# A wait for the gate's weight sums in a graph network's attention

## The chip, the cores and the metric

The kernel runs on one core of a Trainium2 chip. The metric is the time of one execution in device microseconds. Three runs of the kernel before took 2556.47, 2557.34 and 2559.36 us; their median is 2557.34 us.

## The reference

A graph of 1024 nodes with 512 features (all float32) goes through a graph convolution, four transformer layers and a second graph convolution. Around them lie a first normalisation and two residual additions. One layer l, cut to what matters here:

```python
a = attn(ln(h, ln2_w[l], ln2_b[l]), cond, Wq[l], Wk[l], Wv[l], Wo[l])
h = h + a
u = ln(h, ln3_w[l], ln3_b[l]) @ geglu_w[l] + geglu_b[l]   # 512 -> 4096
val, gate = split(u, 2)
h = h + (val * gelu(gate)) @ ffo_w[l] + ffo_b[l]          # 2048 -> 512
```

The attention is a cross attention: the nodes are 16 graphs of 64 nodes each, every graph has its own 256 rows of `cond` (512 features), and keys and values are made from those. There are 8 heads of 64 features. The softmax runs over the 256 rows.

## The kernel before

**The products.** Almost every large product is done by a scheme of Strassen's kind: a 2 x 2 block product takes seven block products in place of eight, in exchange for sums of blocks. Sums of weights are made once per weight. For the keys of one step, `seven` writes seven products into four PSUM banks, named a, b, c and d in the profile (pa_k, pb_k, pc_k, pd_k). PE issues first a, then b, c, d, and then a, c and d again. Between these, other engines take the banks out: ScalarE (ACT) copies a to `s1` (L719), VectorE (DVE) adds b to it (L722, `u_k`), adds c (L725), adds d (L727), and later takes out the second c and d (L733, L735). PE's second product into a bank must wait until the first has been read.

**The attention.** It goes in NG = 8 steps g of two graphs (128 nodes) each. Step g, in the order in which the instructions stand in the program:

- `scores(l, g)`: the score products on PE into four banks, and then, for each bank u, the negated maximum on DVE (L771), the exponentials with their sums on ACT (L776), the reciprocals of the sums on DVE (L779) and two scalings of the probabilities with them on DVE (L781; each is a tensor of 128 x 256 with one factor per row, in place). So a step has eight scalings.
- `kv(l, g + 1)`: keys of the next step (seven products), then a function `between`, then the values of the next step (seven products). So DVE finds the sums of the keys (L722 and on) behind the scalings of this step in its queue.
- `mix(l, g)`: the transposed probabilities times the values.

The function `between` does, in every second step, what is left of two earlier steps: `pair_sums` forms sums of the two steps' outputs on GpSimd (POOL, L846 to L849), and `attn_out_pair` multiplies them with the output projection on PE (banks wab and wcd) and adds the result to h, on DVE (L870 to L881) and POOL (L873, L874, L879, L882). Then DVE makes the next norm's statistics of finished nodes. In step g = NG - 2 = 6 `between` has one task more, ahead of `attn_out_pair`: `geglu_weights(l, 0, *raw)` forms the sums of the first block of the feed-forward part's weights (`wval`, `wgate`, giving `ges`), in four POOL instructions of 128 x 1024 elements (L219 to L222). Their result is first used by PE in the feed-forward part, bank gb. These weights' loads are issued by SP at the beginning of step 6 in program order.

**What sets the order.** Each engine runs its instructions in the order in which the program issues them; between engines semaphores wait for data, and the framework puts those in. The kernel has two means beside: `tc.issue_after` places instructions behind another one in the order, and its own `waiting_for(ins, engine)` gives every instruction that the enclosed code issues on one engine a further dependency, on the instruction `ins`:

Of the kernel before, what the change touches and what calls it, by code (L numbers as in the profile page):

```python
# [14 lines left out]
OP = mybir.AluOpType  # L15
# [8 lines left out]
def gnn_kernel(  # L24
# [26 lines left out]
    nc = tc.nc  # L51
# [29 lines left out]
    @contextmanager  # L81
    def waiting_for(ins, engine):

        traced = nc.cur_bb.bb.instructions
        n = len(traced)
        yield
        for i in traced[n:]:
            if i.engine == engine:
                tc.add_manual_dep(i, ins.ins.name, mybir.DependencyInfo(
                    mybir.DependencyClass.Sync, mybir.DependencyReason.DATA))  # L90

    def bank(name):
        return psum.tile([P, 512], F32, tag="bank", name=name)

    def t512(name, dtype=F32):
        return work.tile([P, 512], dtype, tag="t512", name=name)
# [4 lines left out]
    def slots_of(n, name):  # L101
        return [slot(f"{name}_{i}") for i in range(n)]
# [114 lines left out]
    def sums_of_a(t, a11, a12, a21, a22, s1, s2, s4):  # L217

        t.tensor_tensor(s1, a21, a22, OP.add)  # L219
        t.tensor_tensor(a21, a11, a21, OP.subtract)  # L220
        t.tensor_tensor(s2, s1, a11, OP.subtract)
        t.tensor_tensor(s4, a12, s2, OP.subtract)  # L222
# [37 lines left out]
    def fetch_cond(g):  # L260
        if g < NG:
            raw_conds[g] = [t512(f"cond_{g}_{i}") for i in range(2 * MB)]
            for i, ctile in enumerate(raw_conds[g]):
                nc.sync.dma_start(
                    ctile, cond[2 * g + i // MB, (i % MB) * P:(i % MB + 1) * P, :]
                )
# [19 lines left out]
    conds, left = {}, None  # L286
# [460 lines left out]
    def kv(l, g, wk, wv, between, **also):  # L747
        kT, last_key = keys(l, g, wk)
        between(last_key)
        return kT, values(l, g, wv, **also)  # L750

    def scores(l, g, qT, kT):


        c0 = (g % 4) * P
        probs = []
        banks = [bank(f"sc_{l}_{g}_{u}") for u in range(4)]
        for c2 in range(2):
            for a in range(2):
                for j in range(2):  # L760
                    pj = slice(j * DH, (j + 1) * DH)
                    for b in range(2):
                        with tc.issue_after(mix.last.ins) if g else nullcontext():
                            nc.tensor.matmul(
                                banks[2 * c2 + j][b * NPG:(b + 1) * NPG, a * M:(a + 1) * M],
                                qT[g // 4][c2][pj, a, c0 + b * NPG:c0 + (b + 1) * NPG],
                                kT[c2][pj, a, b * M:(b + 1) * M], start=True, stop=True)
        for u in range(4):
            ps3 = banks[u].rearrange("p (a m) -> p a m", a=2)
            nmax = small.tile([P, 2], F32, tag="nmax", name=f"nmax_{l}_{g}_{u}")  # L770
            nc.vector.tensor_reduce(nmax, ps3, AX.X, OP.max, negate=True)  # L771
            pr = t512(f"pr_{l}_{g}_{u}")
            pr3 = pr.rearrange("p (a m) -> p a m", a=2)
            tot = small.tile([P, 2], F32, tag="tot", name=f"tot_{l}_{g}_{u}")
            for a in range(2):
                nc.scalar.activation(pr3[:, a, :], ps3[:, a, :], AF.Exp,  # L776
                                     bias=nmax[:, a:a + 1], accum_out=tot[:, a:a + 1])
            inv = small.tile([P, 2], F32, tag="inv", name=f"inv_{l}_{g}_{u}")
            nc.vector.reciprocal(inv, tot)  # L779
            for a in range(2):  # L780
                nc.vector.tensor_scalar(pr3[:, a, :], pr3[:, a, :], inv[:, a:a + 1], None, OP.mult)  # L781
            probs.append(pr)
        return probs

# [54 lines left out]
    def pair_sums(l, g, oTs):  # L839

        n = f"{l}_{g}"
        t = nc.gpsimd
        a11, a12, a21, a22 = (halves_of(oT[:, k * M:(k + 1) * M]) for oT in oTs for k in range(2))
        s, more = acc_tile(f"os_{n}"), acc_tile(f"om_{n}")
        s1, s2, s4 = (halves_of(x) for x in (s[:, :M], s[:, M:], more[:, :M]))
        t.tensor_tensor(s1, a21, a22, OP.add)  # L846
        t.tensor_tensor(a21, a11, a21, OP.subtract)
        t.tensor_tensor(s2, s1, a11, OP.subtract)
        t.tensor_tensor(s4, a12, s2, OP.subtract)  # L849
        return [a11, a12, s4, a22, s1, s2, a21], more[:, M:]  # L850

    def attn_out_pair(l, g, left, p1, right):

        n = f"{l}_{g}"
        t = nc.gpsimd
        ab, cd = bank(f"wab_{n}"), bank(f"wcd_{n}")
        a, b, c, d = ab[:, :M], ab[:, M:], cd[:, :M], cd[:, M:]
        h11, h12, h21, h22 = (h[g + i][:, j * M:(j + 1) * M] for i in range(2) for j in range(2))

        def product(i, to, start):  # L860
            multiply(to, left[i], right[i], [(0, P, 0, M)], start)

        kept = acc_tile(f"ou_{n}")
        u2, p7 = kept[:, :M], kept[:, M:]
        product(0, a, True)
        nc.scalar.copy(p1, a)
        product(6, c, True)
        nc.scalar.copy(p7, c)
        product(4, d, False)
        nc.vector.tensor_tensor(h22, d, h22, OP.add)  # L870
        product(5, b, False)
        nc.vector.tensor_tensor(u2, b, p1, OP.add)
        t.tensor_tensor(p7, p7, u2, OP.add)  # L873
        t.tensor_tensor(h22, p7, h22, OP.add)  # L874
        product(1, a, False)
        nc.vector.tensor_tensor(h11, a, h11, OP.add)
        product(3, c, False)
        nc.vector.tensor_tensor(h21, c, h21, OP.add)
        t.tensor_tensor(h21, u2, h21, OP.add)  # L879
        product(2, d, False)  # L880
        nc.vector.tensor_tensor(h12, d, h12, OP.add)  # L881
        t.tensor_tensor(h12, u2, h12, OP.add)  # L882

    def order7(blk, s1, s2, s4):

        return [blk[0], blk[1], s4, blk[3], s1, s2, blk[2]]

    def load_geglu(l, r):
        return [load_w(geglu_w[l][:, r * D:(r + 1) * D], f"wval_{l}_{r}"),
                load_w(geglu_w[l][:, DFF + r * D:DFF + (r + 1) * D], f"wgate_{l}_{r}")]  # L890
# [4 lines left out]
    def geglu_weights(l, r, wval, wgate):  # L895
        s = slots_of(3, f"ges_{l}_{r}")
        sums_of_a(nc.gpsimd, *wval, *wgate, *s)
        return order7([*wval, *wgate], *s)
# [241 lines left out]
    for l in range(L):  # L1140
# [42 lines left out]
        def ln3_norm(*blocks, behind=None):  # L1183
            with tc.issue_after(behind.ins) if behind else nullcontext():
                if blocks:
                    of = [h[nb] for nb in blocks]
                    name = f"ln3_{l}_{blocks[0]}"
                    xns.update(zip(blocks, scaled(of, *moments(of, name), name)))

        def ln3_turn(nb, by=(0, 1)):  # L1190
            turn(xns.pop(nb), ln3T[nb // 4], nb % 4 * P, LN3W + l * KC, LN3B + l * KC,
                 f"ln3_{l}_{nb}", by)
# [8 lines left out]
        for g in range(NG - 1):  # L1201
            kT, v = kv_next
            if g == NG - 2:
                raw = load_geglu(l, 0)
            if l == 0:
                fetch_cond(g + 2)
            probs = scores(l, g, qT, kT)
            ready = [g - 2, g - 1] if g == NG - 2 else [g - 2] if g > 1 else []

            def between(last_key):  # L1210
                nonlocal left
                if len(oTs) == 2:
                    blocks = pair_sums(l, g - 2, oTs)
                    oTs.clear()
                    if g == NG - 2:
                        left = geglu_weights(l, 0, *raw)
                    attn_out_pair(l, g - 2, *blocks, wo7)
                ln3_norm(*ready, behind=last_key)

            if g or l:  # L1220
                kv_next = kv(l, g + 1, wk, wv, between, late=lambda: [ln3_turn(nb) for nb in ready])
            else:
                kv_next = kT_1, values(0, 1, wv)
            save_conds()
            next_cond(l, g + 2)
            for nb in ready:
                if nb >= 4:
                    ln3_sums(nc.gpsimd, nb)
            oTs.append(mix(l, g, probs, v))
# [40 lines left out]
        for r in range(R):  # L1270
# [7 lines left out]
            if r + 1 < R:  # L1278
                raw = load_geglu(l, r + 1)
# [13 lines left out]
            if r + 1 < R:  # L1293
                raw_out = load_out(l, r + 1)
                left = geglu_weights(l, r + 1, *raw)
# [74 lines left out]
```

## Time and profile before

| | |
|---|---|
| median of three runs | 2557.34 us |
| the profiled execution, its own time | 2556.88 us |
| span of the profiled execution | 2555.1 us |
| PE busy (matmuls) | 2516.4 us, 98% of the span |
| DVE busy | 1428.2 us, 56% |
| POOL busy | 646.6 us, 25% |
| ACT busy | 558.0 us, 22% |
| granted clock of PE, mean | 0.996 |

The times in the rows are microseconds from the span's start. A row of a timeline gives the start, the length, the engine, the line of the kernel, the operation and its operands; "x8" says that eight equal instructions that follow each other were merged into one row, and a bracket at the end gives the idle time of the engine before it and what ended it. "PEld" is the loading of weights into PE, which overlaps its matmuls. A name such as pa_k stands for all tiles of that name. "PEclk" or granted clock is the share of PE's full clock that was granted. Layer 0 has its step 6 from about 366 us of the span on, layer 1 from 951, layer 2 from 1545 and layer 3 from 2136.

### The profile page before, as it was taken

To read this page: it belongs to the slowest core of one execution; us is meant where nothing else is said; L and a number is where in the kernel's file an instruction comes from. 1 tells how busy PE (TensorE), PEld (TensorE's weight loads), DVE (VectorE), ACT (ScalarE), POOL (GpSimd) and SP (SyncE) were. 2 spreads that over 40 slices of the span, in tenths; PEclk is the share of its full clock that TensorE was granted. 3 is DMA by queue.
4 is the path that set the end of the run, shared out by engine and by line. 5 is a ranking of instruction groups with operands and counts; after the bars stand their busy time and mean duration, and the time that the engine had idled before them with its cause. 6 is when DMAs were issued, how large, how long until landed. Compare 5 with 4: busy or idle time off the path is not lost. (4 is left out here: it accounts for less than half of the span.)

```text
span 2555.1 us, 32224 instructions
## 1 busy us (share of the span) xinstructions
PE 2516.4 (98%) x12464; PEld 1773.5 (69%) x12464; DVE 1428.2 (56%) x3026; ACT 558.0 (22%) x1318; POOL 646.6 (25%) x539
## 2 busy tenths in 40 slices
PE   8999999999999999999999999999999999999999
PEld 5778886666578886655577887555677887566565
DVE  9655556544664556554474556654475456654561
ACT  7322222111122222111122222111112222211111
POOL 0322234532110012533310003343320002352410
PEclk9999999999999999999999999999999999999999
DMA  5302241111121212010212112110112121111020
GB/s 177 129 38 83 91 139 52 37 50 57 42 83 46 71 34 75 25 54 17 95 38 75 63 63 67 33 54 17 58 66 75 56 77 37 51 33 63 12 87 34
DMA packets 67136, 156.81 MB, mean 61 GB/s; under 512 B 5576, under 2 KB 5904, under 8 KB 66976
## 3 DMA queue, kind: packets, MB, share of 16 engines
q1 hardware_dynamic: 64880, 149.25, 17.9%
q0 software_dynamic: 1376, 4.30, 0.5%
q8 instruction: 103, 1.69, 0.3%
q10 hardware_dynamic: 720, 1.11, 0.1%
q14 instruction: 57, 0.47, 0.1%
HBM read 133.66 MB, written 20.97 MB: 61 GB/s over the span
## 5 line engine op out<-in xcount | busy, mean ns | idle before, releaser
L301 PE MATMUL ga<-ln3T,wval 128*128 128x512 f32 x512 | 233.9, 593 | 0.0
L931 ACT ACTIVATE g<-g,gcols 128x512 f32<-128x512 f32 x128 | 92.3, 721 | 430.9 <-DVE g L944 366.2
L301 PEld LDWEIGHTS ga<-ln3T,wval 128*128 128x128 f32 x512 | 96.0, 190 | 109.9 <-issue 109.1
L776 ACT ACTIVATE pr<-sc,nmax 128x256 f32<-128x256 f32 x256 | 118.2, 474 | 185.4 <-DVE nmax L771 185.4
L846 POOL TENSOR_TENSOR os<-oT 128x256 f32<-128x256 f32 x12 | 8.7, 728 | 566.8 <-DVE oT L821 566.8
L1005 POOL TENSOR_TENSOR hall<-fu,hall 128x512 f32<-128x512 f32 x24 | 30.5, 1270 | 430.5 <-DVE fu L1004 430.5
L301 PE MATMUL pc_k<-ct,wk 128*128 128x256 f32 x512 | 124.8, 388 | 12.4 <-DVE u_k L725 12.4
L301 PE MATMUL pa_v<-wv,ct 128*128 128x256 f32 x512 | 123.1, 379 | 0.0
L301 PE MATMUL pd_k<-ct,wks 128*128 128x256 f32 x512 | 121.9, 381 | 0.0
L301 PE MATMUL fa<-wff,fT 128*128 128x256 f32 x512 | 121.6, 379 | 0.0
L301 PE MATMUL gc<-ln3S,wgate 128*128 128x512 f32 x256 | 120.4, 592 | 1.1 <-DVE gu L941 1.1
L301 PE MATMUL pc_v<-wv,ct 128*128 128x256 f32 x512 | 121.0, 379 | 0.0
L301 PE MATMUL pd_v<-wvs,ct 128*128 128x256 f32 x512 | 121.0, 379 | 0.0
L301 PE MATMUL gd<-ln3T,ges 128*128 128x512 f32 x256 | 120.6, 593 | 0.0
L301 PE MATMUL gb<-ln3S,ges 128*128 128x512 f32 x256 | 120.3, 592 | 0.0
L301 PE MATMUL gc<-ln3T,wgate 128*128 128x512 f32 x256 | 120.3, 592 | 0.0
L301 PE MATMUL gd<-ln3S,ges 128*128 128x512 f32 x256 | 120.3, 592 | 0.0
L301 PE MATMUL pa_k<-ct,wk 128*128 128x256 f32 x480 | 118.0, 389 | 2.1 <-ACT s_k L719 2.1
L301 PEld LDWEIGHTS pc_k<-ct,wk 128*128 128x128 f32 x512 | 99.2, 194 | 27.6 <-DVE u_k L725 13.8
L301 PEld LDWEIGHTS fa<-wff,fT 128*128 128x128 f32 x512 | 97.3, 190 | 21.8 <-issue 9.6
L301 PEld LDWEIGHTS pd_k<-ct,wks 128*128 128x128 f32 x512 | 98.3, 192 | 13.7
L781 DVE TENSOR_SCALAR pr<-pr,inv 128x256 f32<-128x256 f32 x256 | 104.9, 452 | 2.9
(318 smaller groups left out, 4906.0 us busy)
## 6 DMA issues: line engine op xcount, KB each, us to landing
ct<-cond_dram SPq DMA_DIRECT2D x72, 512.0 KB, 4.6
wval<-in_L_gnn_geglu_w_dram SPq DMA_DIRECT2D x32, 512.0 KB, 3.8
wgate<-in_L_gnn_geglu_w_dram SPq DMA_DIRECT2D x32, 512.0 KB, 4.6
wff<-in_L_gnn_ffo_w_dram SPq DMA_DIRECT2D x32, 512.0 KB, 4.7
cond_dram<-ct SPq DMA_DIRECT2D x24, 512.0 KB, 3.0
cond<-in_L_gnn_cond_dram SPq DMA_DIRECT2D x32, 256.0 KB, 4.5
ct<-cond_dram SPq DMA_DIRECT2D x24, 256.0 KB, 4.5
wk<-in_L_gnn_Wk_dram SPq DMA_DIRECT2D x8, 512.0 KB, 5.0
```

Source lines behind the costliest of these rows:

```text
L301: nc.tensor.matmul(at, left[:, k, l0:l1], right[:, k, r0:r1], start=start and n == 0 and k == 0, stop=n == len(cols_of) - 1 and k == 1, sk ...
L776: nc.scalar.activation(pr3[:, a, :], ps3[:, a, :], AF.Exp, bias=nmax[:, a:a + 1], accum_out=tot[:, a:a + 1])
L781: nc.vector.tensor_scalar(pr3[:, a, :], pr3[:, a, :], inv[:, a:a + 1], None, OP.mult)
L846: t.tensor_tensor(s1, a21, a22, OP.add)
L931: nc.scalar.activation(pre, pre, AF.Gelu, bias=gcols[:, cg:cg + 1])
L1005: t.tensor_tensor(h21, halves_of(u2), h21, OP.add)
```

## The change

`scores` keeps its last scaling, and in step 6 `between` puts the four weight sums under `waiting_for` with it. When `between` runs, `scores(l, 6)` has been issued and `scores(l, 7)` has not, so the instruction that is kept is the eighth scaling of step 6. The order of the instructions on each of the five engines is that of before; only the first of the four sums in each layer waits for a further semaphore, DVE's.

```diff
             for a in range(2):
-                nc.vector.tensor_scalar(pr3[:, a, :], pr3[:, a, :], inv[:, a:a + 1], None, OP.mult)
+                scores.last = nc.vector.tensor_scalar(pr3[:, a, :], pr3[:, a, :], inv[:, a:a + 1],
+                                                      None, OP.mult)
             probs.append(pr)
         return probs
...
                     if g == NG - 2:
-                        left = geglu_weights(l, 0, *raw)
+                        with waiting_for(scores.last, mybir.EngineType.Pool):
+                            left = geglu_weights(l, 0, *raw)
                     attn_out_pair(l, g - 2, *blocks, wo7)
```

## The prediction

> **What bounds the kernel now.** I read the page first: busy time by engine. TensorE (PE) works through nearly the whole span, so time is to be had only where PE stands still or runs slow.
>
> ```profile
> span 2555.1 us, 32224 instructions
> PE 2516.4 (98%) x12464; PEld 1773.5 (69%) x12464; DVE 1428.2 (56%) x3026; ACT 558.0 (22%) x1318; POOL 646.6 (25%) x539
> ```
>
> The span less PE's busy time leaves 38.7 us in which PE is idle. The list of PE's waits says for whom; its columns are the total, the number of times and the longest.
>
> ```profile
> PE pc_k L301 <- DVE u_k L725: 12.4, 3, 5.3
> ...
> PE pa_k L301 <- ACT s_k L719: 2.1, 1, 2.1
> ```
>
> Four stalls, 14.5 us, all in the key products. The timeline of PE shows where: in layers 1, 2 and 3, in the attention's step g = 6 (the last but one), between the first product of the keys (pa_k) and the first one of the paired output projection (wab). I quote these two for layer 0, for step 4 of layer 1, then for step 6 of layers 1, 2 and 3 with the stalls between them (start, length, instruction, idle time before it).
>
> ```profile
> 367.46 1.99 PE L301 MATMUL pa_k<-ct,wk 128*128 128x256 f32 x8
> ...
> 376.19 1.89 PE L301 MATMUL pc_k<-ct,wk 128*128 128x256 f32 x8
> 377.92 1.89 PE L301 MATMUL pd_k<-ct,wks 128*128 128x256 f32 x8
> ...
> 379.65 1.03 PE L301 MATMUL wab<-wo,oT 128*128 128x256 f32 x4
> ...
> 886.22 1.99 PE L301 MATMUL pa_k<-ct,wk 128*128 128x256 f32 x8
> ...
> 898.41 1.03 PE L301 MATMUL wab<-wo,oT 128*128 128x256 f32 x4
> ...
> 953.18 1.99 PE L301 MATMUL pa_k<-ct,wk 128*128 128x256 f32 x8
> ...
> 967.41 3.78 PE L301 MATMUL pc_k<-ct,wk 128*128 128x256 f32 x8 [5.33 <-DVE u_k L725]
> ...
> 973.40 1.03 PE L301 MATMUL wab<-wo,oT 128*128 128x256 f32 x4
> ...
> 1546.78 1.99 PE L301 MATMUL pa_k<-ct,wk 128*128 128x256 f32 x8
> ...
> 1556.06 3.66 PE L301 MATMUL pa_k<-ct,wk 128*128 128x256 f32 x8 [2.11 <-ACT s_k L719]
> 1561.43 1.99 PE L301 MATMUL pc_k<-ct,wk 128*128 128x256 f32 x8 [1.71 <-DVE u_k L725]
> ...
> 1564.99 1.03 PE L301 MATMUL wab<-wo,oT 128*128 128x256 f32 x4
> ```
>
> The table by stretches takes the same piece in the four layers, the last one layer 3 (length, then PE busy, weight loads, DVE, ACT, POOL; then the granted clock).
>
> ```profile
> 367.46:379.65 12.19, 12.19 (x61) 10.74 (x57) 7.56 (x19) 5.01 (x18) 7.71 (x7) 1.00 1.01 335
> 953.18:973.40 20.22, 14.89 (x60) 12.31 (x57) 14.84 (x19) 5.01 (x18) 11.41 (x7) 0.83 0.23 64
> 1546.78:1564.99 18.21, 14.39 (x61) 11.66 (x58) 14.97 (x19) 5.01 (x18) 11.36 (x7) 0.91 0.22 64
> 2138.36:2158.21 19.85, 14.51 (x60) 12.08 (x57) 14.84 (x19) 5.01 (x18) 11.41 (x7) 0.83 0.23 61
> ```
>
> The same work takes 12.19 us undisturbed, both in layer 0 and in step 4 of layer 1 (898.41 - 886.22), and 18 to 20 us in the three others. Part of the excess is idle time, part is a slow clock after it: eight matmuls that take 1.89 us take 3.78 and 3.66 behind the gaps.
>
> Why DVE is late there: its own timeline and POOL's in layer 1.
>
> ```profile
> 954.93 2.85 DVE L781 TENSOR_SCALAR pr<-pr,inv 128x256 f32<-128x256 f32 x2
> ...
> 958.37 4.19 DVE L781 TENSOR_SCALAR pr<-pr,inv 128x256 f32<-128x256 f32 x2
> ...
> 962.67 2.57 DVE L781 TENSOR_SCALAR pr<-pr,inv 128x256 f32<-128x256 f32 x2
> ...
> 965.35 0.62 DVE L781 TENSOR_SCALAR pr<-pr,inv 128x256 f32<-128x256 f32 x2
> ...
> 966.67 0.69 DVE L725 TENSOR_TENSOR u_k<-pc_k,u_k 128x512 f32<-128x512 f32 x1
> ```
>
> ```profile
> 955.23 2.40 POOL L219 TENSOR_TENSOR ges<-wgate,wgate 128x1024 f32<-128x1024 f32 x1
> 957.71 2.35 POOL L220 TENSOR_TENSOR wgate<-wval,wgate 128x1024 f32<-128x1024 f32 x1
> 960.02 2.39 POOL L221 TENSOR_TENSOR ges<-ges,wval 128x1024 f32<-128x1024 f32 x1
> 962.49 2.34 POOL L222 TENSOR_TENSOR ges<-wval,ges 128x1024 f32<-128x1024 f32 x1
> ```
>
> Two scalings of probabilities (L781) take 0.62 us alone and up to 4.19 beside the four weight sums: a scaling that meets a running sum gets through only about when that sum ends (at 957.6, 960.1, 962.4 and 964.8). The additions that free PE's banks (L722, L725) queue behind them. The sums are not hurt: 2.34 to 2.40 us each.
>
> **The change, part by part.** It adds one condition, to the four weight sums on POOL in step 6: they wait for the last L781 of that step. No instruction is added, removed or reordered, on any queue; DMA issues and SP's and POOL's queues keep their order.
>
> *Layer 0: nothing.* The lines are POOL's and DVE's there.
>
> ```profile
> 375.23 2.35 POOL L219 TENSOR_TENSOR ges<-wgate,wgate 128x1024 f32<-128x1024 f32 x1 [4.25 <-issue]
> 377.67 2.36 POOL L220 TENSOR_TENSOR wgate<-wval,wgate 128x1024 f32<-128x1024 f32 x1
> ...
> 382.42 2.35 POOL L222 TENSOR_TENSOR ges<-wval,ges 128x1024 f32<-128x1024 f32 x1
> 384.74 0.72 POOL L873 TENSOR_TENSOR ou<-ou 128x256 f32<-128x256 f32 x1
> ...
> 387.26 0.73 POOL L882 TENSOR_TENSOR hall<-ou,hall 128x256 f32<-128x256 f32 x1 [0.33 <-DVE hall L881]
> ```
>
> ```profile
> 372.35 0.62 DVE L781 TENSOR_SCALAR pr<-pr,inv 128x256 f32<-128x256 f32 x2
> ...
> 378.12 0.69 DVE L733 TENSOR_TENSOR kT<-pc_k,u_k 128x512 f32<-128x512 f32 x1 [2.76 <-PE pc_k L301]
> ...
> 382.51 0.42 DVE L872 TENSOR_TENSOR ou<-wab,om 128x256 f32<-128x256 f32 x1 [1.97 <-PE wab L301]
> ```
>
> The last scaling ends at 372.97, the sums begin at 375.23 anyhow (they were idle 4.25 us, which I read as their weights' late arrival). So layer 0 already runs what the change makes of the others, later still. I give times from the start of pa_k (367.46) from here on: last scaling done at +5.5, sums from +7.8 to +17.3.
>
> *Layers 1 to 3: the stalls go.* With POOL silent, the four pairs of scalings take 0.62 us each, and the last is done near +5.5 as in layer 0. L725 then ends well ahead of +8.7, where PE comes to the second pc_k (376.19 in layer 0). So each piece falls to 12.19 us:
> 20.22 - 12.19 = 8.03 (layer 1), 18.21 - 12.19 = 6.02 (layer 2), 19.85 - 12.19 = 7.66 (layer 3), together 21.71 us. Of that 14.5 us is idle time and the other 7.2 the slow clock.
>
> At the clock stands the one place where a page and a row part. In layer 2 a gap of 2.11 us was enough: the next eight matmuls took 3.66 us in place of 1.89. The Trainium skill (TensorE: Matmul & The Clock Gate, section "What's actually happening") says the gate falls to half rate after at least one idle window of about 3.4 us, which the 2.11 us do not fill. The trace does not bear out the plain reading of that rule. By it the slow stretch of layer 2 would have another cause and stay, as the fourth rival below.
>
> *What the wait pushes back.* The sums take 382.42 + 2.35 - 375.23 = 9.54 us, so in layers 1 to 3 they run from about +5.6 to +15.2, not from +2. Behind them in POOL's queue stand the additions of the paired output projection (L873, L874, L879, L882), whose first DVE input (L872) is there at 382.93, that is +15.5, and the last of which feeds the statistics of the next norm. In layer 0 the sums end 2 us later than that and L882 still waited 0.33 us for DVE, and PE lost nothing. Cost: 0. Without that cover (sums ending past about +17.6) each us would be a us on the path.
>
> The sums' results are first used by PE in gb:
>
> ```profile
> 429.95 1.88 PE L301 MATMUL gb<-ln3S,ges 128*128 128x512 f32 x4
> ```
>
> That is 50 us after wab, far beyond a delay of 3.5 us. SP's loads follow PE and DVE, not these sums.
>
> *What the moved sums now lie beside.* No longer L781, but L725, L727, L733 and L735, which read PSUM. Below, the cost is 0: L733 took its 0.69 us in layer 0 beside L220, and a gain is excluded because 12.19 is PE's unbroken time. Above, one sum each, 2.35 us. I take 0, since the row is of the same instructions beside the same sums.
>
> *The sum.* 2556.88 us is the time of the profiled execution (its span is 2555.1). 2556.88 - 21.71 = 2535.2. The median shown, 2557.34, lies 0.46 above; I give 2535.4, between the two. What is late next in these pieces: nothing, PE runs through.
>
> **The rivals.**
> 1. *The moved sums block the additions.* For it: POOL does stop DVE here. Against it: L733 beside L220. If every L725 and L727 waited for the running sum, L725 would wait for the end of L219 (+8.0) and end near +8.7, just in time, and L727 behind L220 near +11.1, some 0.6 us after PE wants its bank at +10.5 (377.92); with L735 and the projection's additions caught too I put it at one sum a layer, 3 x 2.35 = 7 us: 2542.
> 2. *Slower: the sums end too late.* Place: L882 in POOL's queue, then norm and transposes. It costs from an end at about +17.6 on, and outweighs the gain only beyond 21.71/3 = 7.2 us more, when the sums begin after about +15. The wait would have to be let go 10 us after the last scaling, by some later DVE instruction. A release at +20 gives an end at +29.5, 12 us a layer: 36 - 21.7 = 14 slower, 2571. For it: waits are counted by engine, and I can't see the release. Against it: DVE's order puts L781 ahead of all of L722 to L735.
> 3. *It does nothing*, because the weights land after the scalings as in layer 0: 2557. Against it: in layers 1 to 3 the sums start with no idle time ahead of them.
> 4. *The slow stretch of layer 2 stays*: 6.02 - 2.11 - 1.71 = 2.20 us kept, 2537.6. Against it: clock 1.00 in layer 0's same piece, 0.83 and 0.91 only where PE had stood.
>
> **How the numbers follow.** Forecast 0.86, rival 1 0.06, rival 4 0.03, rival 2 0.03, rival 3 0.02. The time is the forecast's, 2535.4. Its own spread is some 1.5 to 3 us, since the three runs before lie between 2556.47 and 2559.36; one sum's length in two layers more above gives 2532.5 to 2541, which holds forecast and rival 4 and the lighter half of rival 1. Faster by over 0.2% (5.1 us, about what a measurement of this kernel can tell from no change): 0.86 + 0.06 + 0.03 = 0.95. Within it: 0.02. Slower: 0.03.
>
> **What would show it.** Right: in layers 1 to 3 every L781 of step 6 is near 0.3 us; the sums start within 0.3 us of the last one's end; pa_k to wab is 12.19 us four times; no wait of PE for L725 is left; PE's idle time is near 24 us; L882's idle time before it is still for L881. Wrong: L725 or L727 longer than 0.7 us beside the sums (rival 1), idle time of DVE's statistics for L882 that grows with PE idle at the transposes (rival 2), sums that start late for another reason, or a new stall further on, as where loads now come too late for a PE that runs 21.7 us ahead.

## The result and the profile after

The changed kernel takes 2533.2 us (median of six runs, 2532.9 to 2534.0); the kernel before takes 2556.9 us (2556.2 to 2559.4, six runs, the three shown above among them). The ratio is 0.991, with a 95% interval of 0.989 to 0.992. The change saves about 23.7 us. The forecast was 2535.4 in a range of 2532.5 to 2541.

The profiled execution took 2532.89 us with a span of 2531.1. The page, busy time by engine:

```profile
span 2531.1 us, 32228 instructions
...
PE 2506.6 (99%) x12464; PEld 1768.6 (70%) x12464; DVE 1403.6 (55%) x3026; ACT 557.3 (22%) x1318; POOL 646.0 (26%) x539
```

The same 12464 matmuls are 9.8 us shorter in sum (2516.4 before), and PE's idle time is 24.5 us in place of 38.7. DVE also lost 24.6 us of "busy" time with the same 3026 instructions, which was waiting booked as work. The list of PE's waits (total, times, longest) has no row for L725 or L719 any more. What is left of it that lies in the layers:

```profile
PE fd L301 <- DVE fs L978: 1.9, 1, 1.9
...
PE gc L301 <- DVE gu L942: 1.1, 1, 1.1
```

(L978 was L977 before: from L782 on the lines of the changed kernel are one higher, from L1217 on two.) The table by stretches, from pa_k to wab in step 6 of layers 0 to 3 (length, then PE busy, weight loads, DVE, ACT, POOL; then the granted clock):

```profile
367.07:379.26 12.19, 12.19 (x60) 10.75 (x57) 7.54 (x19) 5.00 (x18) 7.72 (x7) 1.00 1.00 335
952.62:964.81 12.19, 12.19 (x60) 10.75 (x57) 7.18 (x19) 5.00 (x18) 8.91 (x6) 1.00 0.32 95
1538.18:1550.38 12.20, 12.20 (x61) 10.75 (x58) 7.05 (x19) 5.00 (x18) 8.79 (x6) 1.00 0.32 96
2123.75:2135.94 12.19, 12.19 (x61) 10.75 (x58) 7.18 (x19) 5.00 (x18) 8.91 (x6) 1.00 0.31 96
```

All four pieces are now equal to layer 0's, at full clock, where layers 1 to 3 had 20.22, 18.21 and 19.85. DVE's timeline and then POOL's, layer 1 (pa_k starts at 952.62):

```profile
957.13 0.62 DVE L781 TENSOR_SCALAR pr<-pr,inv 128x256 f32<-128x256 f32 x2
957.66 0.68 DVE L722 TENSOR_TENSOR u_k<-pb_k,s_k 128x512 f32<-128x512 f32 x1
958.45 0.69 DVE L725 TENSOR_TENSOR u_k<-pc_k,u_k 128x512 f32<-128x512 f32 x1
959.83 0.69 DVE L727 TENSOR_TENSOR kT<-pd_k,u_k 128x512 f32<-128x512 f32 x1 [0.69 <-PE pd_k L301]
963.29 0.69 DVE L733 TENSOR_TENSOR kT<-pc_k,u_k 128x512 f32<-128x512 f32 x1 [2.76 <-PE pc_k L301]
...
971.92 0.42 DVE L882 TENSOR_TENSOR hall<-wcd,hall 128x256 f32<-128x256 f32 x1 [1.30 <-PE wcd L301]
```

```profile
957.83 2.35 POOL L219 TENSOR_TENSOR ges<-wgate,wgate 128x1024 f32<-128x1024 f32 x1 [3.12 <-DVE pr L781]
...
965.00 2.35 POOL L222 TENSOR_TENSOR ges<-wval,ges 128x1024 f32<-128x1024 f32 x1
968.24 0.72 POOL L874 TENSOR_TENSOR ou<-ou 128x256 f32<-128x256 f32 x1 [0.89 <-DVE ou L873]
...
972.42 0.73 POOL L883 TENSOR_TENSOR hall<-ou,hall 128x256 f32<-128x256 f32 x1 [1.00 <-DVE hall L882]
```

The last scalings take 0.62 us a pair, the first sum starts 0.08 us after them (957.83 against 957.13 + 0.62), and L722, L725, L727 and L733 run at 0.68 and 0.69 us beside the sums. The sums end at 967.35, and POOL then stands idle 0.89 us until DVE has something for L874.

### The profile page after: what moved, and what is told of

The parts are those of the page before. It is cut to its first block, busy times and chain, and to the rows that moved or that the text cites. A ratio compares the mean times of both kernels' runs of the same rounds, so it can differ in the third digit from the quotient of the medians.

```text
span 2531.1 us, 32228 instructions
## 1 busy us (share of the span) xinstructions
PE 2506.6 (99%) x12464; PEld 1768.6 (70%) x12464; DVE 1403.6 (55%) x3026; ACT 557.3 (22%) x1318; POOL 646.0 (26%) x539
## 3 DMA queue, kind: packets, MB, share of 16 engines
q8 instruction: 103, 1.69, 0.3%
## 5 line engine op out<-in xcount | busy, mean ns | idle before, releaser
L301 PEld LDWEIGHTS pd_k<-ct,wks 128*128 128x128 f32 x512 | 97.3, 190 | 13.2
L301 PEld LDWEIGHTS pd_v<-wvs,ct 128*128 128x128 f32 x512 | 97.3, 190 | 13.2
L301 PEld LDWEIGHTS pc_k<-ct,wk 128*128 128x128 f32 x512 | 97.3, 190 | 13.2
```

The costliest lines, as they stand in the source:

```text
L301: nc.tensor.matmul(at, left[:, k, l0:l1], right[:, k, r0:r1], start=start and n == 0 and k == 0, stop=n == len(cols_of) - 1 and k == 1, sk ...
```

## The experiments

Two things had to be told apart. The theory: a scaling that starts while a weight sum runs is held until that sum ends, and the change helps because the sums move to a stretch in which DVE reads PSUM. Its rivals: the wait works through something else (the order on POOL, the loads), or any later place of the sums does as well. After that came the 2.2 us by which the result lies under the forecast.

**The wait in one layer alone.**

```diff
-                        with waiting_for(scores.last, mybir.EngineType.Pool):
+                        with (waiting_for(scores.last, mybir.EngineType.Pool) if l == 1 else nullcontext()):
```

> The wait stands in layer 1 alone; layers 2 and 3 are as before the change. Theory (each layer's stall comes from its own overlap of weight sums and scalings): layer 1's piece from pa_k to wab goes from 20.22 to 12.19 us, the pieces of layers 2 and 3 stay near 18 to 20 us, the time falls by 8.0 us to about 2549. Rival (the gain hangs together, for instance through the clock or through loads that come earlier everywhere): the pieces of layers 2 and 3 change too, by 2 us or more.

Measured: 2549.80 us (2548.1 to 2550.6) beside 2556.65 for the kernel before, ratio 0.997 (0.996 to 0.998). The stretches of layers 1, 2 and 3:

```profile
952.39:964.58 12.19, 12.19 (x60) 10.75 (x57) 7.19 (x19) 5.00 (x18) 8.91 (x6) 1.00 0.33 91
1537.95:1556.14 18.19, 14.30 (x60) 11.43 (x57) 14.96 (x19) 5.00 (x18) 11.35 (x7) 0.91 0.22 63
2129.52:2149.50 19.98, 14.65 (x60) 12.15 (x57) 14.83 (x19) 5.00 (x18) 11.40 (x7) 0.83 0.22 60
```

Layer 1 has its 12.19, and layers 2 and 3 are within 0.13 us of what they were. The gain is local: layer 1's wait earns layer 1's excess, and the other two pieces do not move by the 2 us that the rival asked for. The medians fell by 6.9 us, a little less than the 8.0 forecast; the span of the profiled execution fell by 8.7 (2555.1 to 2546.4).

**The scalings' source in PSUM, no wait.** The kernel before, but in step 6 the exponentials stay in the score banks and the scaling reads them there. The sums are where they were.

```diff
+                ex = ps3 if g == NG - 2 else pr3
-                nc.scalar.activation(pr3[:, a, :], ps3[:, a, :], AF.Exp,
+                nc.scalar.activation(ex[:, a, :], ps3[:, a, :], AF.Exp,
...
-                nc.vector.tensor_scalar(pr3[:, a, :], pr3[:, a, :], inv[:, a:a + 1], None, OP.mult)
+                nc.vector.tensor_scalar(pr3[:, a, :], ex[:, a, :], inv[:, a:a + 1], None, OP.mult)
```

> No wait. In step 6 the exponentials stay in PSUM and the scalings read them there and write SBUF; the weight sums run beside the scalings as before. Theory (POOL stops only those DVE instructions whose operands are all in SBUF): the scalings take 0.3 to 0.45 us each beside the sums, PE does not wait for L725, the pieces are 12.2 us, the time is 2532 to 2537. Rival (a running sum on POOL slows DVE's scalings whatever they read, or DVE is late for a reason of its queue): scalings of up to 2 us, pieces of 18 to 20 us, 2555 to 2558.

Measured: 2536.12 us (2535.1 to 2537.0), ratio 0.992 (0.990 to 0.993). DVE's timeline in layer 1, the first of POOL's sums, and the stretch:

```profile
958.15 1.64 DVE L782 TENSOR_SCALAR pr<-sc,inv 128x256 f32<-128x256 f32 x4
...
960.37 0.86 DVE L782 TENSOR_SCALAR pr<-sc,inv 128x256 f32<-128x256 f32 x2
```

```profile
956.79 2.35 POOL L219 TENSOR_TENSOR ges<-wgate,wgate 128x1024 f32<-128x1024 f32 x1
```

```profile
954.74:966.93 12.19, 12.19 (x60) 10.75 (x57) 7.88 (x19) 5.16 (x18) 11.35 (x7) 1.00 0.33 91
```

This is the test that carries the theory. The sums start at +2.05 as before, these six scalings run beside them, a pair takes 0.86 us (0.62 with both ends in SBUF and POOL silent, up to 4.19 beside the sums), and the piece is at 12.19. So it is not the time at which the sums run that hurts, but that the scalings read SBUF beside them. (The framework also put L722 ahead of the last two scalings here; that does not touch their lengths, on which the reading rests.) The Trainium skill (SBUF — State Buffer, "Who interferes with whom") describes such an exclusive lock of a port pair that DVE and GpSimd share, with the holder keeping it for its whole instruction; these rows agree. The Trainium skill's list there of the forms that take the lock was not tested row by row.

The kernel is still 2.9 us slower than the changed one. Its profiled execution has a further stall of 1.3 us at gc, in layer 0's feed-forward part at 445.31, and the clock stood at half after the stall of 1.9 us at fd, which cost about 1.7 us and is taken up below. Whether the edit causes the stall at gc is not shown.

**The wait until the last key.** How late may the sums be? Here they wait for L735, the last thing DVE does for the keys.

```diff
+                        with waiting_for(last_key, mybir.EngineType.Pool):
+                            left = geglu_weights(l, 0, *raw)
```

> The sums wait for the last addition of the next keys (L735), about 13 us behind the first pa_k, so they run from about +13 to +23. Theory of the prediction (sums that end past about +17.6 put off the projection's last addition on POOL, the norm and the transposes us for us): in all four layers PE stands still at the transposes or the values by 4 to 5 us and then partly runs at half clock; the stalls at L725 are gone; 2552, between 2548 and 2562. Rival (there is more slack behind, in which the additions disappear): 2533 to 2537.

Measured: 2556.07 us (2554.5 to 2558.0), ratio 0.9997 (0.9987 to 1.0008): the whole gain is gone. PE's waits, POOL's and DVE's timeline in layer 1 (pa_k starts at 958.35), and PE's:

```profile
PE tr_ln L184 <- DVE xn_ln L172: 14.6, 4, 3.7
```

```profile
971.51 2.35 POOL L219 TENSOR_TENSOR ges<-wgate,wgate 128x1024 f32<-128x1024 f32 x1 [11.08 <-DVE kT L735]
...
982.92 0.72 POOL L882 TENSOR_TENSOR hall<-ou,hall 128x256 f32<-128x256 f32 x1
```

```profile
983.67 1.29 DVE L151 BATCH_NORM_STATS2 st_ln<-hall 128x6 f32<-128x512 f32 x2 [5.60 <-POOL hall L882]
```

```profile
989.02 1.93 PE L184 MATMUL tr_ln<-ident,xn_ln 128*128 128x128 f32 x8 [3.65 <-DVE xn_ln L172]
```

The stalls at L725 are gone here too. In their place the projection's last addition (L882) stands behind the sums, DVE's statistics wait 5.60 us for it, and PE's transposes 3.65 us for those, in all four layers. (In this run the framework put one of the four additions, L873, between the third sum and the fourth; the other three stand behind the fourth.) Against the changed kernel the span is 23.3 us longer: PE's idle time grew by 14.1 (2554.4 - 2515.8 = 38.6 against 24.5) and its matmuls by 9.2 us in sum (2515.8 against 2506.6), most of it the slow clock behind the stalls. The time lies within the 2548 to 2562 expected, with stalls of 3.65 us in place of 4 to 5. Between a release at +5.2 and one at +13.2 lies the whole value of the change.

**The sums after the projection.** The other end: the sums behind the paired projection's last POOL addition, so that they stand before nobody in POOL's queue.

```diff
-                    if g == NG - 2:
-                        left = geglu_weights(l, 0, *raw)
                     attn_out_pair(l, g - 2, *blocks, wo7)
+                    if g == NG - 2:
+                        with waiting_for(attn_out_pair.last, mybir.EngineType.Pool):
+                            left = geglu_weights(l, 0, *raw)
```

> The sums wait for POOL's last addition of the projection, so nothing is queued behind them that the norm needs; they run from about +20.6 to +30.2, beside the norm of two nodes' blocks on DVE. Theory (every DVE instruction that has all its operands in SBUF waits for the end of the running sum, the short ones of 128 x 2 too): about one of them gets through per sum, the normalised blocks come 7 us late, PE loses 7 to 10 us in each of the four layers, 2561 to 2573, slower than the kernel before. Rival (short instructions are hardly held, or only the scalings of the probabilities suffer): 2532 to 2540.

Measured: 2564.81 us (2564.1 to 2566.0), ratio 1.003 (1.002 to 1.005), slower than before. PE's waits, DVE's timeline in layer 1 (sums from 980.18 to 989.69) and PE's:

```profile
PE tr_ln L184 <- DVE xn_ln L172: 21.1, 4, 5.3
```

```profile
980.13 1.29 DVE L151 BATCH_NORM_STATS2 st_ln<-hall 128x6 f32<-128x512 f32 x2 [0.84 <-POOL hall L882]
981.34 0.30 DVE L152 BATCH_NORM_AGGREGATE mv_ln<-st_ln 128x2 f32<-128x6 f32 x2
981.67 0.89 DVE L134 TENSOR_SCALAR v_ln<-mv_ln 128x2 f32<-128x2 f32 x1
...
982.79 2.19 DVE L139 SCALAR_TENSOR_TENSOR a_ln<-y_ln,v_ln 128x2 f32<-128x2 f32 x1
984.91 0.68 DVE L722 TENSOR_TENSOR u_v<-pb_v,s_v 128x512 f32<-128x512 f32 x1
985.51 1.78 DVE L141 TENSOR_TENSOR b_ln<-a_ln,y_ln 128x2 f32<-128x2 f32 x1
...
987.52 2.19 DVE L139 SCALAR_TENSOR_TENSOR a_ln<-y_ln,v_ln 128x2 f32<-128x2 f32 x1
...
990.13 0.16 DVE L139 SCALAR_TENSOR_TENSOR a_ln<-y_ln,v_ln 128x2 f32<-128x2 f32 x1
```

```profile
991.88 1.94 PE L184 MATMUL tr_ln<-ident,xn_ln 128*128 128x128 f32 x8 [5.28 <-DVE xn_ln L172]
```

Now the sums meet the next norm's small instructions, all of whose operands are in SBUF. L139 with two elements per partition takes 0.16 us alone and 2.19 beside a sum; L722 between them, which reads PSUM, passes in 0.68. So a small size does not save a DVE instruction, and about one held instruction gets through per sum. The time and PE's loss fit the theory, but its "every" does not hold: the statistics L151 and L152 have their operands in SBUF too, and beside the first sum they take 1.29 and 0.30 us, as in the run before this one with no sum beside them. The reciprocals of the softmax (L779) pass as well, in 0.15 us beside a sum (in the next run, at 961.47). So SBUF operands alone do not decide it, but the operation too: TENSOR_SCALAR, SCALAR_TENSOR_TENSOR and TENSOR_TENSOR with all operands in SBUF were held here, the statistics and the reciprocals were not.

**The wait for half of the scalings.** If holding costs per scaling that meets a sum, letting the sums go after four of the eight should cost less than letting them go at once.

```diff
+                scaling = nc.vector.tensor_scalar(pr3[:, a, :], pr3[:, a, :], inv[:, a:a + 1], None, OP.mult)
+                if u == 1:
+                    scores.last = scaling
```

> The sums wait only for the fourth of the step's eight scalings. Theory (each scaling that begins beside a sum waits for that sum's end): sums from about +3.8 us after pa_k, the second scaling of the third bank and both of the fourth each held, the last done near +11.3, L725 near +12.7; PE stalls some 4 us per layer and may run at half clock behind it, the pieces take 16 to 18 us in layers 1 to 3, 2545 to 2551. Rival (half of the overlap gone, half of the loss gone, or less since half of the banks are done): pieces of 14 to 15.5 us, 2539 to 2544.

Measured: 2559.49 us (2558.2 to 2561.4), ratio 1.0012 (1.0002 to 1.0021): no better than no wait, and both expectations missed. DVE's timeline in layer 1 and the first of POOL's sums:

```profile
956.65 4.90 DVE L781 TENSOR_SCALAR pr<-pr,inv 128x256 f32<-128x256 f32 x2
...
961.66 4.66 DVE L781 TENSOR_SCALAR pr<-pr,inv 128x256 f32<-128x256 f32 x2
```

```profile
956.62 2.35 POOL L219 TENSOR_TENSOR ges<-wgate,wgate 128x1024 f32<-128x1024 f32 x1 [1.67 <-DVE inv L779]
```

The third of POOL's sums runs from 961.36 to 963.75, the last one to 966.17. The four scalings that were left met the four sums one by one, and were held until the last of them ended (961.66 + 4.66 = 966.32). Before, the sums also held DVE for their whole length, but from 955.23 on. My working let one of the four slip in ahead of the first sum, which started 0.03 us earlier than it. Both placements fit one reading: as long as at least as many scalings are left as there are sums, the price is the sums' length, and a later start only moves its end. PE's stall at pc_k grew from 5.33 to 6.0 us in layer 1. By that reading the wait must name the last scaling, or at least one behind the fourth; the places between were not run.

**The same remedy in one more place.** The changed kernel leaves 1.9 us at fd and 1.1 at gc. In the changed kernel's DVE timeline of layer 3's feed-forward part, the sums for the next block (L219 at 2356.40 to L222, ending 2366.76) meet this; below it are the first two of the sums:

```profile
2355.35 1.64 DVE L978 TENSOR_TENSOR fs<-fs,fT 128x512 f32<-128x512 f32 x1
2356.91 2.83 DVE L979 TENSOR_TENSOR fs<-fT,fs 128x512 f32<-128x512 f32 x1
...
2364.59 2.71 DVE L1270 SCALAR_TENSOR_TENSOR base<-xn_again,x_again 128x512 f32<-128x512 f32 x1
```

```profile
2356.40 2.79 POOL L219 TENSOR_TENSOR ges<-wgate,wgate 128x1024 f32<-128x1024 f32 x1
2359.27 2.68 POOL L220 TENSOR_TENSOR wgate<-wval,wgate 128x1024 f32<-128x1024 f32 x1
```

The mean of L979 is 0.78 us over the kernel's 32. In the experiment these sums wait for that L979 as well, in the last layer's last but one block alone:

```diff
-                nc.vector.tensor_tensor(s4, a12, s2, OP.subtract)
+                geglu.last = nc.vector.tensor_tensor(s4, a12, s2, OP.subtract)
...
+                late = last and r == R - 2
-                left = geglu_weights(l, r + 1, *raw)
+                with (waiting_for(geglu.last, mybir.EngineType.Pool) if late else nullcontext()):
+                    left = geglu_weights(l, r + 1, *raw)
```

> The changed kernel with one wait more: in the last layer the feed-forward part's third block leaves POOL's weight sums for the fourth until DVE's last sum of that third block's products is done (the same kind of wait at the other place where PE stands still for DVE). Theory (there DVE's additions with both operands in SBUF, L978, L979 and L1270, wait for running sums, which costs PE 1.1 us in gc and 1.9 us in fd): both stalls go, L979 falls from 2.8 to 0.7 us, the time is about 2530.2, 3.0 us under the changed kernel's 2533.2, and no half-clock stretch can follow there. Rival (the sums now come too late for the fourth block, or beside its own DVE work): a new stall of PE at gb, gd or fd of the fourth block, 2533 or more.

> The changed kernel itself, on the same chip as the one with the second wait, as its yardstick: 2532.5 to 2534.5. Theory of the clock (a stall of 1.9 us at fd halves the clock for 3.4 us in some executions and not in others, by where it falls in a fixed raster of time): executions that differ by up to 1.7 us. Rival (the clock follows the length of the stall alone): they agree within 0.5 us.

Measured on one chip: 2529.65 us (2528.8 to 2530.1) with it, 2533.21 (2532.6 to 2533.6) for the changed kernel again, so 3.6 us less, and the ranges don't meet. To the kernel before the ratio is 0.990 (0.988 to 0.991). POOL's timeline and the costliest groups (mean ns behind the comma):

```profile
2369.04 2.35 POOL L219 TENSOR_TENSOR ges<-wgate,wgate 128x1024 f32<-128x1024 f32 x1 [3.27 <-DVE fs L979]
```

```profile
L979 DVE TENSOR_TENSOR fs<-fT,fs 128x512 f32<-128x512 f32 x32 | 21.9, 684 | 0.0
```

The stalls at fd and gc are gone from the list of PE's waits. They make 3.0 us; the other 0.6 is within the spread of both kernels. This version is the fastest of those run. On the clock the four times of the changed kernel decide nothing: they lie 1.0 us apart, more than the 0.5 of the rival and less than the 1.7 of the theory.

**The kernel before, profiled again.** The terms of the prediction's sum are from one execution. How far do they repeat?

> The kernel before, in a second profiled execution. Theory (the clock is decided in a raster of 3.41 us that runs free of the kernel: the same idle times cost more or less by where they fall): PE's idle times in the three pieces are those of the first profile (5.3, 2.1 and 1.7, 5.3 us), but the pieces' lengths differ from it by up to 1.7 us, and the half clock behind fd is there or not. Rival (the length of a stall decides): 20.22, 18.21 and 19.85 us again within 0.1 us, and the half clock behind fd is there.

Measured: 2557.31 us, span 2555.5. The stretches of layers 1 to 3, and PE's timeline in layer 2:

```profile
952.65:971.84 19.19, 13.86 (x61) 11.62 (x57) 14.83 (x19) 5.00 (x18) 11.40 (x7) 0.91 0.21 59
1545.21:1565.09 19.88, 14.41 (x60) 11.77 (x57) 14.96 (x19) 5.00 (x18) 11.35 (x7) 0.91 0.20 60
2138.46:2158.66 20.20, 14.87 (x61) 12.30 (x58) 14.84 (x19) 5.00 (x18) 11.41 (x7) 0.83 0.21 63
```

```profile
1554.48 1.99 PE L301 MATMUL pa_k<-ct,wk 128*128 128x256 f32 x8 [2.10 <-ACT s_k L719]
1559.85 3.41 PE L301 MATMUL pc_k<-ct,wk 128*128 128x256 f32 x8 [3.37 <-DVE u_k L725]
```

The three pieces stand 7.00, 7.69 and 8.01 us above 12.19, together 22.70 us, and not 21.71 as in the first profile; singly they differ by up to 1.67 us (layer 2: 18.21 and 19.88). In layer 2 pa_k now ran at full speed behind a gap as long as before (2.10 us; 1.99 in place of 3.66). It gained nothing: PE came to pc_k earlier and stood there 3.37 us in place of 1.71, because DVE was late anyway. So the expectation that the idle times repeat failed there, and the slow stretch of layer 2 in the first profile had cost nothing of its own: pc_k starts 14.65 us behind the piece's beginning there and 14.64 here. The lengths differ by up to 1.7 us as the theory had it, and the half clock behind fd is there again.

## Why the prediction was right, and where its sum was short

- *What bounds the kernel, and the mechanism.* Right. Nothing of the 12.19 us is lost in any layer, and the scalings from PSUM show that reading SBUF beside the sums was the cause. Two details were off and cost nothing. Four instructions were added after all (32228 in place of 32224), one semaphore wait on POOL in each layer. And the first pair of scalings takes 0.74 us in layer 1, not 0.62; POOL's last addition of `pair_sums` runs beside it.
- *Layer 0 costs and gains nothing.* Right: 12.19 us before and after; in the changed kernel the list of POOL's waits names the load of wgate ahead of L219, once, 4.2 us.
- *What the wait pushes back, cost 0.* Right. The sums run from +5.2 to +14.7 in layer 1 (said: +5.6 to +15.2), and the last addition still waits 1.00 us for DVE, not the other way.
- *What the moved sums lie beside, cost 0.* Right: L725 and L727 at 0.69 us. Rival 1 is out.
- *Rival 2, the sums too late.* Its mechanism is real and lay 8 us off: with the release at +13.2 its place and its waits are as described, and the gain is gone. Its price was reckoned over three layers, 21.71/3 = 7.2 us each, but the wait stands in layer 0 too, and there the late sums cost as much. Over four layers the gain is used up at 5.4 us each; in that run the sums ended at +23.2, 5.6 us past the +17.6, and the loss was 23.3/4 = 5.8 us a layer. That is about a us for a us, as said, though only 3.65 of it is idle time and the rest mostly slow clock. Rival 3 is out by the 23.7 us.
- *Rival 4, the slow stretch of layer 2 stays.* Out: that piece runs at clock 1.00. Its 2.20 us were no separate cost: in the second profile of the kernel before, the same pa_k ran at full speed and PE stood longer at pc_k instead. For the same reason the split of the 21.71 us into 14.5 idle and 7.2 slow is that execution's own.
- *The sum.* The three pieces gave 21.71 us as worked out, but the spans differ by 24.0. Two terms were left out of it. One is worth 1.69 us and lies in the feed-forward part of layer 3, behind the stall of 1.9 us at fd, which the change does not touch: from the fd stall's matmuls to fa the first profile shows 12.48 us (2392.18 to 2404.66), the changed kernel 10.79 (2369.90 to 2380.69), by the clock alone. The other, 0.56 us, lies before layer 1's step 6 (pa_k at 953.18 and 952.62), of which layer 0's pa_k has 0.39 already (367.46 and 367.07). 2556.88 - 21.71 - 1.69 - 0.56 = 2532.92, and 2532.89 was measured. That the change removes the 1.69 by more than chance is not shown. Both profiles of the kernel before have the half clock there and both of the changed kernel do not, but the same stall kept it in the runs of one layer, PSUM and half of the scalings, and lost it in those of the last key and of the sums after the projection, which both gained nothing.

The step that fell short is therefore the last one: a sum over pieces from a single execution was set against that execution's own time, as if the rest of the kernel repeated to 0.1 us. The range, from the spread of the runs, covered it, with 0.7 us to spare at its lower end.

## What to carry to other kernels

In this kernel long GpSimd work is best put beside stretches of VectorE that read PSUM. Look for VectorE instructions whose duration varies several-fold with GpSimd busy beside them, since their waiting counts as busy time. Release the GpSimd work with the last VectorE instruction that it would hold: a wait for half of them was worth nothing here, and a wait 8 us too long gave back all of the gain through the instructions behind it in GpSimd's queue. Then ask what the next such meeting is; one more wait of this kind, in one place, was worth 3.6 us.

## What the runs showed of the hardware

**The clock falls on a fixed raster, and a little over half a window of idle time was enough.** In the profiles, stretches at half clock inside the kernel last 3.41 or 6.83 us. In the kernel before they start at 965.54, 1556.05, 2149.97 and 2395.73 us, which is 173, 174 and 72 times 3.4133 us apart, so they lie on one raster of 3.41 us. Where that raster lies against the kernel differs between executions: an edge splits the changed kernel's stall at fd into 0.55 and 1.35 us in its first profile, into 0.62 and 1.28 in its second. The windows of the raster around the fd stall, first the kernel before (granted clock third from the end):

```profile
2392.31:2395.73 3.42, 1.52 (x8) 1.02 (x7) 3.42 (x4) 0.59 (x1) 3.34 (x4) 1.00 0.00 0
2395.73:2399.14 3.41, 3.41 (x10) 2.70 (x9) 1.25 (x2) 0.00 (x0) 1.68 (x2) 0.50 0.00 0
```

Then the kernel after:

```profile
2367.63:2371.04 3.41, 2.86 (x14) 2.17 (x12) 3.27 (x4) 1.17 (x2) 3.33 (x3) 1.00 0.22 77
2371.04:2374.45 3.41, 2.06 (x10) 1.83 (x11) 3.41 (x4) 0.00 (x0) 3.33 (x3) 1.00 0.00 0
2374.45:2377.87 3.42, 3.42 (x17) 3.02 (x16) 1.35 (x3) 0.00 (x0) 2.00 (x3) 1.00 0.00 0
```

Before, all 1.9 us of the gap lie in one window (3.42 - 1.52), and the next runs at 0.50. After, an edge of the raster splits the gap into 0.55 and 1.35 us, and the clock stays at 1.00. Nine profiles of this case have this stall. In the five in which it lies within one window half clock followed; in the four in which an edge splits it, with at most 1.60 us on one side, none did. From layer 0's attention to the end of the layers, windows at full clock with 1.89 us of idle PE or more were followed by half clock, and those with 1.71 or less were not. It is no rule for the whole kernel: among the graph convolution's small products, the run with the wait in layer 1 alone has a window with 1.99 us idle (83.16 to 86.57) and full clock behind it. The Trainium skill (TensorE: Matmul & The Clock Gate, "What's actually happening") gives a free-running window of 3413 ns, with which the raster agrees; its idle window of about 3.4 us, read as one wholly idle, does not agree with a fall after 1.9 us. What a stall of 1.9 to 3.4 us costs thus depends on where it falls: the same one at fd cost 1.9 us in one execution and about 3.6 in another. This is read from the records of the executions profiled; no run moved a stall across an edge on purpose.

**A held VectorE instruction waits for one GpSimd instruction, not for the series.** Between two sums that follow each other within 0.1 us, one held instruction gets through, then the next sum holds the next one.

**GpSimd can be held too.** The sums of step 6 take 2.34 to 2.40 us in all ten profiles, beside scalings of about 0.3 us. In the feed-forward part of layer 3 of the changed kernel, L219 took 2.79 us and L220 2.68: a VectorE addition of 0.68 us that had itself been held (L978 until 2356.99, L979 until 2359.74) was still running when each of them began.
